# A two-layer attention and mixture-of-experts kernel: finer layernorm and exponential steps, routers called in fewer steps, and the first layer's tiles woven in from the third quarter

## The chip, the cores and the metric

The kernel runs on one core of one Trainium2 chip. The metric is the device time of one execution in microseconds (us). The kernel before took 978.13 us in the median of three runs (972.77 to 980.31).

## What is computed

All in float32. The input x has 16 x 256 tokens of 128 channels. Four residual steps follow one another, and each begins with a layernorm of x:

```python
x = x + attn_a(layernorm(x))   # 16 heads of 8, softmax inside blocks of 64 tokens
x = x + ffn(layernorm(x))      # router, top 2 of 8 experts, hidden 512, silu(g) * u
x = x + attn_b(layernorm(x))   # 16 heads over the 16 sequences of one position, plus a band bias
x = x + ffn(layernorm(x))      # the same experts again
```

The expert step needs, for each token, the two largest of eight router logits, a softmax over these two, and the two experts' outputs weighted by it.

## The kernel before, in words

**Tiling.** The 256 positions are cut in four quarters (q = 0 to 3). A quarter has 1024 tokens, which lie in SBUF as `xq[q]`, 8 groups of 128; a half is four groups. "Layer 0" is attn_a with its ffn, "layer 1" attn_b with its ffn. For each quarter a layer does its attention in two halves (`attention_a`, L397, or `attention_b`, L487), and after both halves a `router` (L585).

**Attention.** `prepare_a` and `prepare_b` make the layernorm, turn it on TensorE (PE), and make queries and keys. `attention_a` does for each group: values, then for two blocks scores on PE (L411), the row maximum (L419) and the subtraction (L420) on VectorE (DVE); then one exponential of both blocks on ScalarE (ACT, L425), transposes of the blocks (L430), their copies (L434), the product with the values (L441), the division, and an add into `xq` on GpSimd (POOL, L449). `attention_b` has the same order of work for a pair of groups, with one exponential at L535. `layernorm_t` (L266) is the layernorm of all: BN statistics of four groups, a power on POOL, the scaling of four groups, the transposes; it yields after each of these.

**Experts.** `router` makes logits, chooses two experts per token, counts, and gets each token's row in a table sorted by expert. It then scatters 16 x 128 rows to `sorted_in` in device memory by indirect DMAs of POOL (L694). `tile_tables` builds lists of tiles of 256 rows, each of one expert; it runs among the scatters. A list knows the rows of the first two quarters, the next one of the third, the last one of all. `experts` works through 39 tiles of a layer: fetch of rows (`xin`) and of three weight pieces (`w`) by SP two tiles ahead, transposes of the rows (`xt`, L889), the products g and u (L947), tanh (L952), two DVE operations (L953, L955), the product down (`acc`, L897), transposes and weighting, and a scatter to `results` (L920). Each tile is two units (`units`). `combine` reads `results` back and adds them to `xq`.

**Order of the work.** All these are Python generators. `weave(main, *sides)` steps through an attention half (24 steps in layer 0, 20 in layer 1) and calls the side generators in proportion: a side of `count` calls is spread over the first `n` steps. The sides are the router of the quarter before, the preparation of the next half, and units of experts. A scheduler below the kernel then settles each engine's final order from this program order and the dependencies. `behind_now` adds a dependency: a layernorm's or router's operation is put behind the last subtraction (`beat`) issued so far. In layer 0 units begin with quarter 3 (7 units by the end of its first half, 15 by the end of its second); the last router is run with a unit at every second call, and units then go on to number 52. In layer 1 units of layer 0 fill the first three quarters (`GOAL`), and layer 1's own begin behind quarter 2.

```python
CHOSEN = 10                       # the router's calls before its first scatter
ROUTER = CHOSEN + TOP * NG + 4    # 30 calls in all
sides = [(routing, ROUTER // 2 if half == 0 else ROUTER, n)]
```

Of the kernel before, what the change touches and what calls it, by code (L numbers as in the profile page):

```python
# [25 lines left out]
NQ = T // BS  # L26
# [4 lines left out]
TOP = 2  # L31
# [79 lines left out]
def hybrid_kernel(  # L111
# [154 lines left out]
    def layernorm_t(q, halves, name, put, keep=None, own=None):  # L266
        mv = p2.tile([P, NG, 2], F32, tag="mv", name=f"mv_{name}")
        rstd = p2.tile([P, NG], F32, tag="rstd", name=f"rs_{name}")
        ln = {}
        for half in halves:  # L270
            gs = range(4 * half, 4 * half + 4)
            stats = p2.tile([P, 4, 6], F32, tag="stats", name=f"st_{name}_{half}")
            for i, g in enumerate(gs):
                behind_now(nc.vector.bn_stats(out=stats[:, i, :], in_=xq[q][:, g, :]))
                nc.vector.bn_aggr(out=mv[:, g, :], in_=stats[:, i, :])
            some = slice(4 * half, 4 * half + 4)
            veps = p2.tile([P, 4], F32, tag="veps", name=f"ve_{name}_{half}")
            arrived[0] = nc.vector.tensor_scalar(veps, mv[:, some, 1], EPS, None, ALU.add).ins
            nc.gpsimd.tensor_tensor(rstd[:, some], veps, minus_half[:, some], ALU.pow)
            yield  # L280
        for half in halves:
            if keep is None:
                ln[half] = p2.tile([P, 4, C], F32, tag="ln", name=f"ln_{name}_{half}")
            for g in range(4 * half, 4 * half + 4):
                behind_now(
                    nc.vector.tensor_scalar(
                        ln[half][:, g % 4, :] if keep is None else keep(g),
                        xq[q][:, g, :], mv[:, g, 0:1], rstd[:, g : g + 1],
                        ALU.subtract, ALU.mult,
                    )  # L290
                )
            if own is not None:
                own(half)
            yield
        for half in halves:
            pt = psum(f"lnp_{name}_{half}")
            for i in range(4):
                g = 4 * half + i
                nc.tensor.transpose(
                    pt[:, i * P : (i + 1) * P],  # L300
                    ln[half][:, i, :] if keep is None else keep(g), ident,
                )
            put(half, pt)
            yield
# [92 lines left out]
    def attention_a(q, half):  # L397
        lnT, qT, kx = ready.pop((q, half))
        for g in range(4 * half, 4 * half + 4):
# [7 lines left out]
            for b in range(2):  # L407
                sc = ps_sc.tile([P, 512], F32, tag="sc", name=f"sc_{n}_{b}")
                blk = 2 * (g % 4) + b
                for v in range(2):  # L410
# [10 lines left out]
                    ex[:, b], sc3, mx[:, 0:8].unsqueeze(2).to_broadcast([P, 8, BS]),  # L421
                    ALU.subtract,
                ).ins
                yield
            nc.scalar.activation(ex, ex, AF.Exp)  # L425
            eT = p2.tile([P, 2, 4, P], F32, tag="eT", name=f"eT_{n}")
            for b in range(2):
                pt = psum(f"t_{n}_{b}")
# [58 lines left out]
    def attention_b(q, half):  # L487
# [15 lines left out]
        for dg in range(2 * half, 2 * half + 2):  # L503
# [7 lines left out]
            for gg in range(2):  # L511
# [3 lines left out]
                for j in range(4):  # L515
# [15 lines left out]
                beat[0] = nc.vector.tensor_tensor(  # L531
                    ex[:, gg], sb, mx.unsqueeze(2).to_broadcast([P, H, 32]), ALU.subtract
                ).ins
                yield
            nc.scalar.activation(ex, ex, AF.Exp)  # L535
            for gg in range(2):
                g = 2 * dg + gg
                n = f"B{q}_{g}"
# [313 lines left out]
    def experts(layer):  # L852
        def fetch(li, i):
# [9 lines left out]
                in_=sorted_in[layer][bass.ds(row, TT)].rearrange("(p b) r -> p (b r)", b=2),  # L863
            )
            known = [put for q in range(LISTED + li) for put in after[layer, q]]
            key = f"rows_{layer}"
            tc.declare_no_dep(
                got.ins, group=key, keep=known, reason="rows that the list did not know"
# [139 lines left out]
    def units(layer, upto):  # L1008
        while unit[layer] < upto:
            unit[layer] += 1  # L1010
            next(tiles[layer])
            yield

    def run(gen):
        for _ in gen:
            pass


    def weave(main, *sides):
        taken = [0] * len(sides)  # L1020
        for k, _ in enumerate(main):
            for i, (side, count, n) in enumerate(sides):
# [3 lines left out]
        for i, (side, count, n) in enumerate(sides):  # L1026
# [12 lines left out]
    FIRST = BEGIN[0] + BEGIN_B - 3  # L1039
    GOAL = [FIRST + (BEGIN[2] - FIRST) * (k + 1) // 3 for k in range(3)]  # L1040
    GOAL += [BEGIN[2] + (UNITS - BEGIN[2]) * (k + 1) // 3 for k in range(3)]

    for layer in range(2):
        tiles[layer], unit[layer] = experts(layer), 0
        if layer == 0:
            first = prepare_a(0, 0)
            next(first)
            for some in late:
                follow(some.ins, arrived)
            run(first)  # L1050
        else:
            weave(begin_b(0), (units(0, FIRST), FIRST - unit[0], BEGIN_B))
        routing = iter(())
        for q in range(NQ):
            for half in range(2):
                n = STEPS[layer]
                sides = [(routing, ROUTER // 2 if half == 0 else ROUTER, n)]
                last = (q, half) == (NQ - 1, 1)
                if layer == 0:
                    main = attention_a(q, half)  # L1060
                    if not last:
                        sides.append((prepare_a(q + half, 1 - half), 5, 2 * n // 3))
                else:
                    main = attention_b(q, half)
                    if half == 0:
                        sides.append((prepare_b(q, 1), 3, n // 2))
                    elif q < NQ - 2:
                        sides.append((begin_b(q + 1), BEGIN_B, 4 * n // 5))
                if q == NQ - 1:
                    goal = BESIDE * (1 + half) // 2  # L1070
                    goal = max(goal, unit[layer])
                    sides.append((units(layer, goal), goal - unit[layer], n))
                elif layer == 1:
                    goal = GOAL[2 * q + half]
                    sides.append((units(0, goal), goal - unit[0], n))
                weave(main, *sides)
                if layer == 1 and half == 1:
                    finish_b(q)
                    if q == NQ - 2:
                        n = BEGIN_B - 3  # L1080
                        run(routing)
                        weave(begin_b(q + 1), (units(1, n), n, BEGIN_B))
            run(routing)
            routing = router(layer, q)
# [49 lines left out]
```

## Time and profile before

| what | value |
|---|---|
| median of the runs, us | 978.13 (972.77 to 980.31, three runs) |
| the profiled execution's own time, us | 1056.63 |
| its span, us | 1054.9 |
| mean granted TensorE clock | 0.911 |
| PE busy | 901.1 us (85%) |
| DVE busy | 619.6 us (59%) |
| ACT busy | 397.6 us (38%) |
| POOL busy | 361.1 us (34%) |
| DMA moved | 107.69 MB, 102 GB/s in the mean |

The profile is of one execution. Busy time is the time in which an engine worked on an instruction. PE is TensorE's matmuls and PEld its weight loads, which overlap them; each float32 matmul is two records. PEclk is the share of full clock granted to TensorE. Idle time before an instruction is put down to what released it last. The first 330 us are layer 0's attention: quarters 1, 2 and 3 begin near 74, 156 and 235 us; the last router of layer 0 and its remaining tiles follow up to about 455 us. The adds into `xq` (L449) mark the ends of the groups.

### The profile page before, as it was taken

Reading aid. Unit: us, or ns where it says so; the run is one execution under the profiler, and the core shown is the slowest. Engines: PE = TensorE matmul, PEld = TensorE weight load, DVE = VectorE, ACT = ScalarE, POOL = GpSimd, SP = SyncE. Lnnn points to the kernel's source line nnn. Section 1 sums busy time; section 2 is a strip of 40 time slices with the busy share of each in tenths; the row PEclk is TensorE's granted clock in tenths of the full one; section 3 lists DMA queues with packets and bytes.
Section 4 is the critical chain, followed back from the end, with each engine's and each line's share of the span. In section 5 each row is a group of like instructions: output and inputs, shape, how many; then the busy total and the mean of one; then the engine's idle time right before and its main releaser. Section 6 shows DMA issues by size and latency. Waiting matters only on the chain.

```text
span 1054.9 us, 17640 instructions
## 1 busy us (share of the span) xinstructions
PE 901.1 (85%) x5992; PEld 733.6 (70%) x5992; DVE 619.6 (59%) x1749; ACT 397.6 (38%) x773; POOL 361.1 (34%) x404
## 2 busy tenths in 40 slices
PE   5987897989989979989887789588976997999993
PEld 3765666768778758877765667467765776887872
DVE  4676357557746745577766447546754674456452
ACT  2442243244434323436444254233622332443431
POOL 2121522442443463341112631442225345333322
PEclk9997787689989999999997889898978988999997
DMA  7000000041333545673121211133203444568772
GB/s 198 3 2 1 29 14 1 21 127 41 99 101 106 151 149 166 196 225 96 42 81 41 65 58 42 61 95 127 81 14 109 121 134 148 170 192 253 222 213 88
DMA packets 104922, 107.69 MB, mean 102 GB/s; under 512 B 10688, under 2 KB 80320, under 8 KB 104832
## 3 DMA queue, kind: packets, MB, share of 16 engines
q1 hardware_dynamic: 95024, 87.36, 27.8%
q0 software_dynamic: 9088, 18.89, 5.1%
q8 instruction: 48, 0.79, 0.3%
q10 hardware_dynamic: 720, 0.30, 0.1%
q14 instruction: 42, 0.34, 0.1%
HBM read 83.38 MB, written 23.13 MB: 101 GB/s over the span
## 4 chain that ended last, share of the span: by engine, by line
PE 66%; DVE 12%; DMA 6%; another core or an unknown queue 5%; ACT 5%; issue 4%; POOL 1%; SPq 1%; ACTq 0%; POOLq 0%; DVEq 0%
PE g L947 11%; PE acc L897 10%; PE u L947 10%; PE o_A L441 6%; PE sc_A L411 6%; PE t_A L430 3%; PE v_B L354 3%; PE o_B L554 2%; DMA back<-results 2%; PE sc_B L517 2%; DMA xin<-sorted_in 2%; DMA results<-yo,to 2%; PE v_A L354 2%; PE lg_F L599 1%
## 5 line engine op out<-in xcount | busy, mean ns | idle before, releaser
L920 POOL DMA_INDIRECT results<-yo,to x156 | 154.1, 988 | 299.7 <-ACT yo L913 269.3
L897 PE MATMUL acc<-h,w 128*128 128x256 f32 x624 | 174.3, 401 | 12.1 <-DVE h L955 9.1
L947 PE MATMUL g<-xT,w 128*128 128x256 f32 x624 | 171.5, 394 | 4.4 <-issue 2.7
L947 PE MATMUL u<-xT,w 128*128 128x256 f32 x624 | 169.8, 393 | 3.8 <-DVE th L953 2.0
L952 ACT ACTIVATE th<-g 128x512 f32<-128x512 f32 x156 | 93.6, 600 | 203.8 <-PE g L947 132.1
L953 DVE SCALAR_TENSOR_TENSOR th<-th,g 128x512 f32<-128x512 f32 x156 | 106.4, 683 | 105.6 <-ACT th L952 84.0
L694 POOL DMA_INDIRECT sorted_in<-rows,pos_i_F x128 | 125.0, 977 | 124.7 <-issue 38.4
L897 PEld LDWEIGHTS acc<-h,w 128*128 128x128 f32 x624 | 121.6, 200 | 36.4 <-DVE h L955 14.8
L947 PEld LDWEIGHTS g<-xT,w 128*128 128x128 f32 x624 | 119.0, 198 | 23.0 <-issue 4.9
L947 PEld LDWEIGHTS u<-xT,w 128*128 128x128 f32 x624 | 115.7, 196 | 20.4 <-issue 3.4
L955 DVE TENSOR_TENSOR h<-th,u 128x512 f32<-128x512 f32 x156 | 106.6, 684 | 21.6 <-remote 5.6
L411 PE MATMUL sc_A<-k_A,q_A 128*128 128x256 f32 x256 | 86.4, 456 | 19.0 <-DVE ex_A L420 14.1
L441 PEld LDWEIGHTS o_A<-va,eT_A 128*64 128x64 f32 x1024 | 63.6, 147 | 20.4 <-issue 8.4
L411 PEld LDWEIGHTS sc_A<-k_A,q_A 128*128 128x128 f32 x256 | 50.8, 225 | 33.2 <-DVE ex_A L420 16.3
L441 PE MATMUL o_A<-va,eT_A 128*64 128x18 f32 x1024 | 67.7, 219 | 5.6 <-issue 3.1
L905 ACT COPY yT<-acc 128x256 f32<-128x256 f32 x78 | 29.0, 372 | 100.6 <-PE acc L897 89.2
L419 DVE TENSOR_REDUCE mx_A<-sc_A 128x8 f32<-128x512 f32 x64 | 43.1, 681 | 35.5 <-PE sc_A L411 34.8
L434 ACT COPY eT_A<-t_A 128x512 f32<-128x512 f32 x64 | 36.6, 589 | 67.9 <-PE t_A L430 61.8
L449 POOL TENSOR_TENSOR xq<-xq,att_A 128x128 f32<-128x128 f32 x32 | 14.6, 456 | 130.5 <-DVE att_A L373 120.1
L913 ACT ACTIVATE yo<-y,xin 128x128 f32<-128x128 f32 x156 | 48.6, 366 | 20.4 <-PE y L908 10.6
L425 ACT ACTIVATE ex_A<-ex_A 128x1024 f32<-128x1024 f32 x32 | 34.0, 1064 | 42.5 <-DVE ex_A L420 31.0
L430 PEld LDWEIGHTS t_A<-k_sb,ex_A 128*128 128x128 f32 x256 | 34.0, 159 | 20.7 <-issue 10.4
(173 smaller groups left out, 1318.0 us busy)
## 6 DMA issues: line engine op xcount, KB each, us to landing
w<-in_wg SPq DMA_DIRECT2D x78, 256.0 KB
w<-in_wu SPq DMA_DIRECT2D x78, 256.0 KB
w<-in_wd SPq DMA_DIRECT2D x78, 256.0 KB
xin<-sorted_in SPq DMA_DIRECT2D x78, 132.0 KB
back<-results SPq DMA_DIRECT2D x16, 512.0 KB
results<-yo,to POOLq DMA_INDIRECT x156
sorted_in<-zero SPq DMA_DIRECT2D x2, 1056.0 KB
sorted_in<-rows,pos_i_F POOLq DMA_INDIRECT x128
```

Of the source, the lines that this page charges most:

```text
L354: nc.tensor.matmul(pv[:, a * P : (a + 1) * P], lhsT=src[:, g * n + a].rearrange("p r k -> p (r k)"), rhs=w, start=True, stop=True,)
L411: nc.tensor.matmul(sc[:, v * 4 * BS : (v + 1) * 4 * BS], lhsT=qT[:, blk, 2 * v : 2 * v + 2, :].rearrange("p r k -> p (r k)"), rhs=kx[:, :, ...
L430: nc.tensor.transpose(pt[:, i * P : (i + 1) * P], ex[:, b, 2 * i : 2 * i + 2, :].rearrange("p h k -> p (h k)"), ident,)
L441: nc.tensor.matmul(po[b * BS : (b + 1) * BS, i * 18 : (i + 1) * 18], lhsT=eT[:, b, 2 * v + i % 2, u * BS : (u + 1) * BS], rhs=vt[:, b, 2 * ...
L694: put_row = nc.gpsimd.indirect_dma_start(out=sorted_in[layer], out_offset=bass.IndirectOffsetOnAxis(ap=pos_i[:, k, g : g + 1], axis=0), in ...
L897: nc.tensor.matmul(acc[:, 0:TT], lhsT=w[:, 2, hc * P : (hc + 1) * P], rhs=h[:, j * TT : (j + 1) * TT], start=(hc == 0), stop=(hc == NHC - 1),)
L913: nc.scalar.activation(y[:, b, :], py[:, b * P : (b + 1) * P], AF.Identity, scale=t[:, b, C : C + 1],)
L920: put_row = nc.gpsimd.indirect_dma_start(out=results[layer], out_offset=bass.IndirectOffsetOnAxis(ap=to[:, b : b + 1], axis=0), in_=y[:, b ...
L947: nc.tensor.matmul(p[:, j * TT : (j + 1) * TT], lhsT=w[:, k, hs], rhs=xT, start=True, stop=True,)
L952: nc.scalar.activation(th, pg, AF.Tanh, scale=0.5)
L953: nc.vector.scalar_tensor_tensor(th, th, 1.0, pg, ALU.add, ALU.mult)
L955: beat[0] = nc.vector.tensor_tensor(h, th, pu, ALU.mult).ins
```

## The change

`layernorm_t` yields after two groups of statistics and after two groups of scaling, where it yielded after four. The exponentials of `attention_a` and `attention_b` are made for each block right after its subtraction, where one instruction covered two blocks. `weave` takes a first and a last step for each side. The router has 34 calls in place of 30 (the layernorm has four more); 25 are made beside the first half (15 before) and 9 in the first third of the second half. The preparation of a half of layer 0 has 7 calls for 5, `begin_b` 15 for 11. Units of layer 0 begin in the second half of quarter 2, from its 12th step on: 3 by its end, 8 and 13 by the ends of quarter 3's halves (before: 0, 7 and 15). In layer 1 the two halves of quarter 3 have the goals 8 and 13 (before 8 and 15).

```diff
@@ layernorm_t
-            for i, g in enumerate(gs):
+            for i in range(4):
+                g = 4 * half + i
                 behind_now(nc.vector.bn_stats(out=stats[:, i, :], in_=xq[q][:, g, :]))
                 nc.vector.bn_aggr(out=mv[:, g, :], in_=stats[:, i, :])
+                if i == 1:
+                    yield
...
-            for g in range(4 * half, 4 * half + 4):
+            for i in range(4):
+                g = 4 * half + i
                 behind_now(
                     nc.vector.tensor_scalar(
...
                 )
+                if i == 1:
+                    yield
@@ attention_a
                     ALU.subtract,
                 ).ins
+                nc.scalar.activation(ex[:, b], ex[:, b], AF.Exp)
                 yield
-            nc.scalar.activation(ex, ex, AF.Exp)
@@ attention_b
+                nc.scalar.activation(ex[:, gg], ex[:, gg], AF.Exp)
                 yield
-            nc.scalar.activation(ex, ex, AF.Exp)
@@ the plan
-    CHOSEN = 10
+    CHOSEN = 14
...
-                while taken[i] < min(count * (k + 1) // n, count):
+                while taken[i] < min(count * max(k + 1 - first, 0) // (last - first), count):
...
-    BEGIN_B = 2 + 6 + 3
-    FIRST = BEGIN[0] + BEGIN_B - 3
+    BEGIN_A, BEGIN_B = 5 + 2, 2 + 10 + 3
+    AHEAD = 8
+    FAST = ROUTER * 3 // 4
+    FIRST = BEGIN[0] + AHEAD
...
+    OWN = {5: BESIDE // 4, 6: BESIDE * 5 // 8, 7: BESIDE}
...
-                sides = [(routing, ROUTER // 2 if half == 0 else ROUTER, n)]
...
-                if q == NQ - 1:
-                    goal = BESIDE * (1 + half) // 2
+            if half == 0:
+                sides = [(routing, FAST, 0, n)]
+            else:
+                sides = [(routing, ROUTER - FAST, 0, n // 3)]
+            if layer == 0:
+                main = attention_a(q, half)
+                if hq + 1 < 2 * NQ:
+                    sides.append((prepare_a((hq + 1) // 2, 1 - half), BEGIN_A, 0, 2 * n // 3))
+                wanted, goal = 0, OWN.get(hq, 0)
...
+                wanted, goal = (0, GOAL[hq]) if q < NQ - 1 else (1, OWN[hq])
+            goal = max(goal, unit[wanted])
+            first = n // 2 if layer == 0 and hq == 5 else 0
+            sides.append((units(wanted, goal), goal - unit[wanted], first, n))
+            weave(main, *sides)
```

More of the change, by code (lines that the diff above doesn't have):

```diff
@@ L270, in layernorm_t @@
         for half in halves:
-            gs = range(4 * half, 4 * half + 4)
             stats = p2.tile([P, 4, 6], F32, tag="stats", name=f"st_{name}_{half}")
-            for i, g in enumerate(gs):
+            some = slice(4 * half, 4 * half + 4)
+            for i in range(4):
+                g = 4 * half + i
                 behind_now(nc.vector.bn_stats(out=stats[:, i, :], in_=xq[q][:, g, :]))
                 nc.vector.bn_aggr(out=mv[:, g, :], in_=stats[:, i, :])
-            some = slice(4 * half, 4 * half + 4)
+                if i == 1:
+                    yield
             veps = p2.tile([P, 4], F32, tag="veps", name=f"ve_{name}_{half}")
@@ L283, in layernorm_t @@
                 ln[half] = p2.tile([P, 4, C], F32, tag="ln", name=f"ln_{name}_{half}")
-            for g in range(4 * half, 4 * half + 4):
+            for i in range(4):
+                g = 4 * half + i
                 behind_now(
                     nc.vector.tensor_scalar(
-                        ln[half][:, g % 4, :] if keep is None else keep(g),
+                        ln[half][:, i, :] if keep is None else keep(g),
                         xq[q][:, g, :], mv[:, g, 0:1], rstd[:, g : g + 1],
@@ L865, in fetch @@
             known = [put for q in range(LISTED + li) for put in after[layer, q]]
+            assert len(known) == (LISTED + li) * TOP * NG
             key = f"rows_{layer}"
@@ L1021, in weave @@
         for k, _ in enumerate(main):
-            for i, (side, count, n) in enumerate(sides):
-                while taken[i] < min(count * (k + 1) // n, count):
+            for i, (side, count, first, last) in enumerate(sides):
+                while taken[i] < min(count * max(k + 1 - first, 0) // (last - first), count):
                     taken[i] += 1
                     next(side, None)
-        for i, (side, count, n) in enumerate(sides):
+        for i, (side, count, _, _) in enumerate(sides):
             for _ in range(count - taken[i]):
@@ L1047, in hybrid_kernel @@
             next(first)
+            next(first)
             for some in late:
@@ L1051, in hybrid_kernel @@
         else:
-            weave(begin_b(0), (units(0, FIRST), FIRST - unit[0], BEGIN_B))
+            weave(begin_b(0), (units(0, FIRST), FIRST - unit[0], 0, BEGIN_B))
         routing = iter(())
-        for q in range(NQ):
-            for half in range(2):
-                n = STEPS[layer]
-                sides = [(routing, ROUTER // 2 if half == 0 else ROUTER, n)]
[L1058 to L1068, printed above, removed]
-                if q == NQ - 1:
-                    goal = BESIDE * (1 + half) // 2
[L1071 to L1082, printed above, removed]
@@ new lines, in hybrid_kernel @@
+        n = STEPS[layer]
+        for hq in range(2 * NQ):
+            q, half = hq // 2, hq % 2
+            if half == 0:
[7 more added lines that the diff above has]
+                wanted, goal = 0, OWN.get(hq, 0)
+            else:
+                main = attention_b(q, half)
+                if half == 0:
+                    sides.append((prepare_b(q, 1), 3, 0, n // 2))
+                elif q < NQ - 2:
+                    sides.append((begin_b(q + 1), BEGIN_B, 0, 4 * n // 5))
+                wanted, goal = (0, GOAL[hq]) if q < NQ - 1 else (1, OWN[hq])
[3 more added lines that the diff above has]
+            weave(main, *sides)
+            if half == 0:
+                continue
@@ L1083, in hybrid_kernel @@
             run(routing)
+            if layer == 1:
+                finish_b(q)
+                if q == NQ - 2:
+                    weave(begin_b(q + 1), (units(1, AHEAD), AHEAD, 0, BEGIN_B))
             routing = router(layer, q)
```

## The prediction, made before the changed kernel was run

> **What bounds the kernel now.** I read the page's first two parts, then the table by stretches, the groups, PE's own waits and the timeline. The page says which engine fills the span and what it was granted:
>
> ```profile
> PE 901.1 (85%) x5992; PEld 733.6 (70%) x5992; DVE 619.6 (59%) x1749; ACT 397.6 (38%) x773; POOL 361.1 (34%) x404
> PEclk9997787689989999999997889898978988999997
> ```
>
> TensorE (PE) is the bound, but its clock falls below full in slices 4 to 8. The profiled execution took 1056.63 us (span 1054.9), 78.5 us over the median of 978.13. In its chain of waits 4.9%, some 52 us, is put on "another core or an unknown queue"; one core runs, so I take this and the cold clock after it for the profile's own cost. The first such piece starts at 126.5 us; what lies before it should be in the timed runs too. The table by stretches (length; busy PE, PEld, DVE, ACT, POOL; clock; DMA) gives attention halves of layer 0:
>
> ```profile
> 48.50:74.30 25.80, 23.67 (x215) 18.08 (x213) 17.22 (x50) 11.54 (x17) 4.08 (x6) 1.00 0.00 1
> 74.30:123.70 49.40, 40.46 (x254) 30.93 (x253) 27.26 (x95) 15.12 (x22) 14.31 (x17) 0.72 0.03 11
> 155.80:205.30 49.50, 40.48 (x253) 31.21 (x252) 31.32 (x123) 15.14 (x22) 13.24 (x15) 0.72 0.03 9
> 205.30:234.50 29.20, 26.41 (x212) 20.19 (x211) 17.17 (x51) 11.64 (x17) 14.43 (x17) 0.88 0.38 119
> 234.50:282.40 47.90, 46.48 (x337) 38.42 (x336) 35.92 (x121) 21.61 (x39) 15.15 (x18) 1.00 0.16 51
> 403.00:458.00 55.00, 55.00 (x273) 48.24 (x272) 27.54 (x47) 22.58 (x59) 18.99 (x20) 1.00 0.61 187
> ```
>
> A half alone takes 25.8 us. A half beside a router (rows two and three) has 39 more matmul records and takes 23.6 us more. At clock 0.72, 28% of the time is missing: 0.28 x 49.4 = 13.8 us. Idle grows from 2.1 to 8.9 us; the rest, 3.0 us, is the router's own matmuls. With expert tiles beside it (row five) the same work runs at clock 1.00. PE's waits name the idle:
>
> ```profile
> PE sc_A L411 <- DVE ex_A L420: 14.1, 13, 3.2
> PE t_B L541 <- ACT ex_B L535: 4.7, 2, 4.5
> PE rank_F L662 <- DVE runs L649: 3.4, 1, 3.4
> PE rank_F L662 <- issue: 3.3, 1, 3.3
> ```
>
> and the timeline shows two such holes, the scores held by VectorE (DVE) and the ranks held by the router's chain:
>
> ```profile
> 86.40 2.93 PE L411 MATMUL sc_A<-k_A,q_A 128*128 128x256 f32 x6 [2.49 <-DVE ex_A L420]
> 102.50 0.66 PE L662 MATMUL rank_F<-taken_F,k_late 128*128 128x64 f32 x2 [3.34 <-issue]
> ```
>
> [...] after the 3.34 us hole at 99.2 the same 4 transposes take 1.06 us at 106.0, against 0.60 at 98.6. [...]
>
> **A: exponentials block by block.** Removed: 32 ACTIVATEs of 1064 ns (L425) and 16 of 1059 (L535). Added: 96 of half the size. The tanh of 128x512 (L952) takes 600 ns, so a pair costs 1200: (1200 - 1062) x 48 = 6.6 us more on ACT, hidden since ACT is busy 38%. Without that cover it would be 6.6 us of the end at most. Gain: the first block's transposes no longer wait for the second subtract (684 ns) and half the exponential (464 ns), so start 1.15 us earlier. That matters only where PE is waiting: in the order in which the built programs' instructions stand, t_A_1_0 now stands before the last matmul of sc_A_2_0, in the 2.49 us hole, and there are two such holes. Some 1 us each, and 1 us of the 4.5 us wait of t_B: -3 us. Bounds: 0, and -14 (the waits for ex_A and ex_B, 18.8 us, three quarters gone).
>
> **B: layernorms by two groups.** No instruction is added; four groups' BN statistics are 4 x (272 + 165) ns = 1.7 us, now in runs of 0.9. In the built order the first router has 26 instructions between mx_A_1_0 and the subtract that follows it before, 28 after: that burst (76.0 to 81.1 us) isn't shortened. But the subtract of the second block of group 0 now stands ahead of two groups' statistics, and two ln rows move behind two subtracts. I take 0.4 us in each of 8 routers: -3 us; bounds 0 and -8. That finer steps do no more is what I read from the order.
>
> **C: routers in fewer groups.** CHOSEN 10 to 14 is the same work in more calls, so ROUTER is 34 for 30. The first half makes 25 calls in place of 15, so 11 scatters in place of 5, at 962 ns and 0.30 us between: 6 x 1.26 = 7.6 us of POOL move forward. Behind them on POOL stand the adds of att into xq (455 ns), which nothing needs before the next router. DVE's choice takes 14/25 x 24 = 13.4 steps of attention in place of 10/15 x 24 = 16. The rank hole: in the new order no PE work stands between v_A_2 and rank, while before k_A_1 and t_A_2_0 (1.06 + 0.60 us) did. DVE's va, 0.42 us, then about 16 links of the chain follow v_A_2; 17 links with four k_A and a va took 5.1 us at 97.3 (3.05 without those), so 0.18 each and 2.9 us. With 0.38 us from v to va the hole is about 3.7 us against 3.34. The four k_A (0.42 us each in sequence) now stand behind the router's positions, covered by q_A's scaling on ACT (2.79 us); uncovered, 1.7 us. Sum: +1 us over the routers of quarters 0 and 1; bounds -4 and +10.
>
> **D: tiles beside the third quarter.** Pair-steps (units) of layer 0 go from 0, 7, 8, 15 (last half of quarter 2, two halves of quarter 3, last router) to 3, 5, 5, 17. A tile takes 5.07 us in the dense stretch (ten from 402.8 to 453.5), so a unit 2.54. PE's work is the same; the gain is what falls into idle time. Quarter 2's last half has 2.8 us idle and 0.12 x 29.2 = 3.5 us lost to clock: I take 3. Two more units beside the last router fall into its 10.0 us idle (330 to 403): 3. The new risk: xt of tile 0 now stands near t_A_6. Its rows need all 32 scatters. Four of these stand after the add of group 4, which was at 211.8 us: 5.1 us, 2.5 to land (220.4 to 223.0 before), one xin fetch 2.1 (issued 223.1, used 225.3): 221.5, against about 222 for t_A_6. No slack, so +1 for a stall. SP's later fetches (two tiles ahead) and weights come sooner by as much; only tile loads are queued there. Sum -5; bounds -12 and +8.
>
> **E: cold clock.** From 14 to 330 us the missing clock is 0.28 x 49.4 + 0.16 x 32.1 + 0.28 x 49.5 + 0.12 x 29.2 + 0.07 x 47.7 = 40 us. The rank holes stay, so the cold stretch behind each stays. I take a fifth of the rest, 36 us, for A and B together beyond the 3.5 in D: -7. Bounds: +6 and -30.
>
> **F: layer 1.** begin_b has 15 steps for 11, the units beside it are the same 8; the order hardly changes: -1; bounds -10 and +10.
>
> Sum: -3 -3 +1 -5 -7 -1 = -18 us. In the profiled execution's time 1056.6 - 18 = 1039; against the median 978.1 - 18 = 960 us.
>
> **The rivals.** (1) The cold stretches of the two router quarters go altogether: for this speaks row five, clock 1.00 with the same router; against it the rank hole. Another 20 us of E: 940. (2) The holes only move: the burst of 26 to 28 instructions stays, dense stretches stay at 55.00 of 55.00; it does not do what it says, and A and D alone leave 975. (3) Slower: the compressed routers. If DVE's denser choice lengthens the hole per router by the uncovered k_A, 1.7 us, and draws one more 6.8 us cold stretch (3.4 lost) in the six routers that run beside attention: 6 x 5.1 = +31, against -18 gives +13: 991. It decides from 3 us per router. Against it: DVE is busy 27.3 of 49.4 us there.
>
> **How the numbers follow.** My forecast has 0.45, its own range 948 to 970; rival 1 0.22, rival 2 0.20, rival 3 0.13. The 8-in-10 range reaches from 936 (rival 1, with A at its far bound) to 989. A measurement can tell about 1%, 968.3 to 987.9. Faster: 0.43 + 0.22 + 0.02 = 0.67. Same: 0.02 + 0.17 + 0.03 = 0.22. Slower: 0.01 + 0.10 = 0.11.
>
> **What would show it.** A: twice the exponentials, near 600 ns, and t_A or t_B less often behind ACT. B: waits of sc_A for ex_A below 14.1 us. C: rank_F still waiting over 3 us in quarters 1 and 2. D: g of tile 0 before the last half of quarter 2 ends, xt's wait for xin there under 3 us, clock there 1.00. E: mean clock above 0.911, router halves under 47 us. Wrong: a stall at the first xt over 5 us, router halves longer than 49.5 us, or rank holes gone.

## The result

| what | before | after |
|---|---|---|
| median, us (20 runs each, same series) | 981.26 (972.77 to 988.16) | 974.12 (970.42 to 978.74) |
| ratio | | 0.9925 [0.9905, 0.9945] |
| profiled execution, us | 982.37 | 974.5 |
| its span, us | 980.6 | 972.7 |
| mean granted TensorE clock | 0.942 | 0.949 |

The change makes the kernel 0.75% faster, some 7 us. The forecast was 18 us. Ratios in this document leave out executions more than 1.5% above the fastest of the same kernel, so a ratio can differ from that of the two medians. The profile that the forecast was read from was of an execution 78 us longer than the timed runs; the kernel was profiled again (run before_again), and that execution of 982.37 us is the "before" of this section and the next.

### The profile page after: what moved, and what is told of

It reads as the page before. It is cut to its first block, busy times and chain, and to the rows that moved or that the text cites. A ratio compares the mean times of both kernels' runs of the same rounds, so it can differ in the third digit from the quotient of the medians.

```text
span 972.7 us, 17640 instructions
## 1 busy us (share of the span) xinstructions
PE 856.2 (88%) x5992; PEld 706.9 (73%) x5992; DVE 619.7 (64%) x1749; ACT 402.2 (41%) x821; POOL 358.6 (37%) x404
## 4 chain that ended last, share of the span: by engine, by line
PE 68%; DVE 11%; DMA 8%; ACT 5%; POOL 3%; issue 3%; SPq 0%; ACTq 0%; POOLq 0%; DVEq 0%
PE g L953 12%; PE u L953 11%; PE acc L903 11%; PE o_A L446 6%; PE sc_A L416 5%; DMA back<-results 3%; PE t_A L435 3%; PE v_B L359 2%; PE o_B L559 2%; PE sc_B L522 2%; DMA results<-yo,to 2%; POOL sorted_in L699 2%; PE v_A L359 2%; DMA sorted_in<-rows,pos_i_F 2%; ACT q_A L333 2%
## 5 line engine op out<-in xcount | busy, mean ns | idle before, releaser
L903 PE MATMUL acc<-h,w 128*128 128x256 f32 x624 | 166.2, 385 | 6.4 <-DVE h L961 6.2
L953 PE MATMUL u<-xT,w 128*128 128x256 f32 x624 | 165.3, 384 | 3.8 <-DVE th L959 3.8
L953 PE MATMUL g<-xT,w 128*128 128x256 f32 x624 | 166.3, 386 | 0.9 <-ACT xT L897 0.5
L903 PEld LDWEIGHTS acc<-h,w 128*128 128x128 f32 x624 | 116.7, 192 | 26.3 <-DVE h L961 10.4
L953 PEld LDWEIGHTS g<-xT,w 128*128 128x128 f32 x624 | 117.0, 193 | 17.3 <-issue 1.6
L953 PEld LDWEIGHTS u<-xT,w 128*128 128x128 f32 x624 | 112.3, 192 | 18.9 <-DVE th L959 6.0
L416 PE MATMUL sc_A<-k_A,q_A 128*128 128x256 f32 x256 | 80.1, 423 | 20.4 <-DVE ex_A L425 13.1
L416 PEld LDWEIGHTS sc_A<-k_A,q_A 128*128 128x128 f32 x256 | 45.8, 206 | 30.4 <-DVE ex_A L425 12.4
L429 ACT ACTIVATE ex_A<-ex_A 128x512 f32<-128x512 f32 x64 | 40.1, 634 | 47.0 <-DVE ex_A L425 46.7
L359 PE MATMUL v_B<-wi_sb,xt_B 128*128 128x128 f32 x256 | 37.0, 298 | 24.0 <-DVE att_B L378 23.1
```

The costliest lines, as they stand in the source:

```text
L359: nc.tensor.matmul(pv[:, a * P : (a + 1) * P], lhsT=src[:, g * n + a].rearrange("p r k -> p (r k)"), rhs=w, start=True, stop=True,)
L416: nc.tensor.matmul(sc[:, v * 4 * BS : (v + 1) * 4 * BS], lhsT=qT[:, blk, 2 * v : 2 * v + 2, :].rearrange("p r k -> p (r k)"), rhs=kx[:, :, ...
L903: nc.tensor.matmul(acc[:, 0:TT], lhsT=w[:, 2, hc * P : (hc + 1) * P], rhs=h[:, j * TT : (j + 1) * TT], start=(hc == 0), stop=(hc == NHC - 1),)
L953: nc.tensor.matmul(p[:, j * TT : (j + 1) * TT], lhsT=w[:, k, hs], rhs=xT, start=True, stop=True,)
```

## The profile after

First the busy shares and the granted clock in 40 slices, from the page of the kernel before, profiled again:

```profile
PE 861.1 (88%) x5992; PEld 708.5 (72%) x5992; DVE 620.2 (63%) x1749; ACT 397.3 (41%) x773; POOL 360.1 (37%) x404
PEclk9998998699999999999998879997999999999997
```

and from the page of the changed kernel:

```profile
PE 856.2 (88%) x5992; PEld 706.9 (73%) x5992; DVE 619.7 (64%) x1749; ACT 402.2 (41%) x821; POOL 358.6 (37%) x404
PEclk9999879789999999999999879989999999999997
```

The work is the same: 5992 matmul records, 48 more ACTIVATEs and 4.9 us more of them on ACT. Both pages have their weak places where layer 0 runs beside its routers (slices 4 to 9) and where layer 1 does so (slices 22 to 24). The table by stretches (length; busy PE, PEld, DVE, ACT, POOL; clock; DMA share; GB/s) gives for the kernel before the four halves of quarters 1 and 2 of layer 0, and then the second quarter of layer 1:

```profile
73.50:118.00 44.50, 34.88 (x258) 26.75 (x258) 28.41 (x102) 15.61 (x23) 14.31 (x16) 0.88 0.03 11
118.00:146.50 28.50, 24.82 (x204) 18.16 (x204) 16.48 (x45) 11.45 (x17) 13.09 (x16) 0.94 0.07 24
146.50:194.90 48.40, 39.28 (x252) 31.05 (x253) 31.44 (x126) 15.22 (x22) 13.23 (x15) 0.75 0.03 9
194.90:220.80 25.90, 23.59 (x213) 17.72 (x211) 17.53 (x50) 11.53 (x17) 14.40 (x17) 1.00 0.33 108
...
517.70:600.40 82.70, 63.27 (x571) 52.19 (x570) 51.25 (x153) 32.72 (x54) 30.56 (x30) 0.86 0.16 52
```

and for the changed kernel the same stretches:

```profile
77.60:119.20 41.60, 33.72 (x281) 26.05 (x279) 28.00 (x105) 15.92 (x27) 19.11 (x22) 0.92 0.06 19
119.20:150.60 31.40, 27.07 (x187) 20.51 (x186) 16.13 (x39) 12.09 (x20) 8.18 (x12) 0.84 0.03 11
150.60:195.20 44.60, 37.65 (x261) 29.20 (x259) 31.29 (x132) 16.08 (x27) 16.11 (x18) 0.81 0.04 13
195.20:228.90 33.70, 30.38 (x224) 23.98 (x223) 17.82 (x44) 14.02 (x25) 11.17 (x14) 0.90 0.32 99
...
516.50:596.20 79.70, 60.07 (x558) 49.78 (x557) 49.13 (x151) 33.09 (x59) 29.50 (x30) 0.85 0.18 54
```

In quarters 1 and 2 the first halves became 3 to 4 us shorter and the second halves 3 to 8 us longer; the sum of the four is 147.3 us before and 151.3 after. Quarter 3, which has ten units of tiles beside it for fifteen, went from 90.1 to 81.9 us. Layer 0 as a whole, to the first read of its results, took 419.7 us and takes 421.9. Layer 1's attention went from 348.5 to 336.7 us, and its second quarter is still a stretch with a clock of 0.85 and 19.6 us without matmul. TensorE's own waits in the changed kernel (total, times, longest, us) say what stands there:

```profile
PE v_B L359 <- DVE att_B L378: 23.1, 2, 12.6
...
PE rank_F L667 <- DVE runs L654: 3.5, 1, 3.5
PE rank_F L667 <- issue: 3.5, 1, 3.5
```

against these in the kernel before:

```profile
PE lnp_B L299 <- DVE vb L360: 10.5, 1, 10.5
...
PE ot_B L495 <- DVE att_B L373: 8.2, 2, 6.2
...
PE t_B L541 <- ACT ex_B L535: 4.6, 2, 4.5
...
PE rank_F L662 <- DVE runs L649: 3.4, 1, 3.4
PE rank_F L662 <- issue: 2.9, 1, 2.9
```

The two rank holes of layer 0 (TensorE's waits for what the ranks are counted from) stayed: 2.9 and 3.4 us before, 3.5 us each after. The wait for the exponential of two blocks (t_B, 4.5 us) is gone. And two waits in layer 1, of 10.5 and 6.2 us, became two of 12.6 and 10.5. These last two are named v_B <- att_B, but att_B is short work (0.29 us): what was late is seen one engine further, in the timeline. Lines of it for the changed kernel around both waits, engine by engine:

```profile
545.09 0.96 POOL L699 DMA_INDIRECT sorted_in<-rows,pos_i_F  x1 [5.90 <-DVE pos_i_F L692]
...
564.02 0.96 POOL L699 DMA_INDIRECT sorted_in<-rows,pos_i_F  x1 [0.30 <-DMA sorted_in<-rows,pos_i_F]
565.00 1.05 POOL L281 TENSOR_TENSOR rs_B<-ve_B,minus_half 128x4 f32<-128x4 f32 x1
...
548.27 0.27 DVE L280 TENSOR_SCALAR ve_B<-mv_B 128x4 f32<-128x4 f32 x1
...
566.09 1.28 DVE L289 TENSOR_SCALAR ln_B<-xq,mv_B,rs_B 128x128 f32<-128x128 f32 x4 [10.07 <-POOL rs_B L281]
...
571.50 2.05 PE L359 MATMUL v_B<-wi_sb,xt_B 128*128 128x128 f32 x8 [12.63 <-DVE att_B L378]
...
651.21 0.16 DVE L924 TENSOR_TENSOR to<-xin,no_pads 128x2 int32<-128x2 f32 x1 [11.60 <-DMA xin<-sorted_in]
...
652.64 2.05 PE L359 MATMUL v_B<-wi_sb,xt_B 128*128 128x128 f32 x8 [10.49 <-DVE att_B L378]
```

The variance of the next quarter's layernorm (ve_B) is ready at 548.5 us. Its power (rs_B) starts on POOL at 565.0, because 16 scatters of the router stand before it, 0.96 us each and 0.30 between, some 20 us from 545.1. VectorE's scaling waits 10.07 us for the power and then 2.34 us for that of the second half, the attention's att_B stands behind both in VectorE's order, and TensorE waits 12.63 us for att_B. The second wait has another head: `to`, which a tile makes from its fetched rows, stands early in VectorE's order and waits 11.60 us for a fetch of layer 1's first tile. That fetch needs the last scatter of the next router, which starts on POOL at 646.58 us; SP issues the fetch at 649.05.

The kernel before has the same first wait under another name (lnp_B <- vb). There 12 of the 16 scatters stand before the first power; the second one, for which VectorE waits 6.14 us more, starts at 572.29 behind three others and two scatters of a tile. Lines of its timeline:

```profile
563.88 0.96 POOL L694 DMA_INDIRECT sorted_in<-rows,pos_i_F  x1 [0.31 <-issue]
564.86 1.05 POOL L279 TENSOR_TENSOR rs_B<-ve_B,minus_half 128x4 f32<-128x4 f32 x1
...
573.37 2.94 DVE L286 TENSOR_SCALAR ln_B<-xq,mv_B,rs_B 128x128 f32<-128x128 f32 x4 [6.14 <-POOL rs_B L279]
```

## The experiments

In the expectations, "GpSimd queue" (theory 1 in the first eight) is the theory that bunched scatters hold what stands behind them on GpSimd, and that the routers' fast pace so gives the gain of the other parts back. "Holes only move" (theory 2) is its rival: the waits belong to VectorE's own chains and go elsewhere when one is removed. Ratios are against the kernel before on the same chip, with 95% intervals.

| run | median, us | ratio |
|---|---|---|
| exp_alone | 976.74 | 0.9934 [0.9911, 0.9957] |
| layernorm_alone | 965.54 | 0.9818 [0.9769, 0.9867] |
| pace_alone | 998.39 | 1.0162 [1.0107, 1.0217] |
| tiles_alone | 991.56 | 1.0089 [1.0059, 1.0120] |
| exp_and_layernorm | 954.69 | 0.9709 [0.9658, 0.9760] |
| fast_pace_without_tiles | 977.72 | 0.9946 [0.9924, 0.9969] |
| after_old_pace | 954.24 | 0.9750 [0.9691, 0.9809] |
| after_old_pace_layer1 | 963.62 | 0.9833 [0.9782, 0.9885] |
| after_to_behind | 965.92 | 0.9859 [0.9807, 0.9912] |
| fast_pace_power_on_vector | 969.30 | 0.9763 [0.9693, 0.9833] |
| slow_choice_fast_scatters | 978.27 | 0.9980 [0.9959, 1.0001] |
| old_choice_fast_scatters | 1035.52 | 0.9901 [0.9867, 0.9936] |
| old_choice_fast_scatters_2 | 972.04 | 0.9893 [0.9859, 0.9927] |
| old_pace_to_behind | 955.47 | 0.9701 [0.9653, 0.9749] |
| exp_layernorm_to_behind | 953.83 | 0.9684 [0.9636, 0.9731] |
| exp_layernorm_to_behind_power | 948.92 | 0.9661 [0.9621, 0.9701] |
| exp_layernorm_to_behind_power_all | 949.54 | 0.9679 [0.9641, 0.9718] |

**before_again** is the kernel before, with a new profile.

> The kernel before, profiled once more, since its first profile was 78 us longer than its runs. Theory 1 (the queue of GpSimd: the changed routers bunch 16 scatters, DVE then waits for a power or for a tile's rows behind them, 23 us of PE idle time in two places) expects a span near 980 us without a PE wait over 6 us in layer 1. Theory 2 (holes only move: the kernel before has waits of the same kind and sum) expects 15 us or more of PE waits behind scatters in layer 1 here too. Both expect the two rank holes of 3.4 us near 99 and 181 us.

982.37 us. The 10.5 us wait is there, so "no wait over 6 us in before" of the GpSimd-queue view was a miss: the wait isn't new with the change, it became 2 us longer.

**The old pace**, everywhere or in layer 1 alone:

```diff
-            if half == 0:
-                sides = [(routing, FAST, 0, n)]
-            else:
-                sides = [(routing, ROUTER - FAST, 0, n // 3)]
+            sides = [(routing, ROUTER // 2 if half == 0 else ROUTER, 0, n)]
```

> The changed kernel with the routers at their old pace (half of the calls beside the first half, the rest over the first half of the second). Theory 1 expects 945 to 962 us, ratio 0.965 to 0.98 to before: the 12.6 and 10.5 us waits of v_B shrink by more than half. Theory 2 expects the time of the changed kernel within 0.5%, 969 to 979 us.

> The changed kernel with the old pace in layer 1 alone. Theory 1, both waits lie in layer 1: 945 to 962 us, within 0.4% of the run with the old pace everywhere. If the fast pace costs or gains in layer 0, the two runs differ by more. Theory 2: 969 to 979 us.

954.24 and 963.62 us. The fast pace costs the changed kernel some 17 us (0.9925 to 0.975), about 9 of them in layer 1. The intervals of the two old-pace runs overlap, so layer 0's share of some 8 us is less sure; the GpSimd-queue view had expected 0.4% between the two at most, a miss. In the trace of the first both rank holes of layer 0 and the 12.6 us wait are gone. The second wait, which that view expected to shrink by more than half, stayed at 9.5 us.

**The tile's places behind.** The changed kernel, with `to` tied to the last subtraction issued (the expectation calls it the product h):

```diff
-                nc.vector.tensor_tensor(to, t[:, :, C + 1], elsewhere, ALU.max)
+                behind_now(nc.vector.tensor_tensor(to, t[:, :, C + 1], elsewhere, ALU.max))
```

> The changed kernel with one dependency more: DVE's operation that reads a tile's row numbers (to, from xin) is put behind the last product h, so it can't stand early in DVE's queue and hold it until xin lands. Theory 1 expects the 10.5 us wait at 642 us to go and 6 to 16 us to be won: 958 to 968 us. Theory 2 expects another wait in its place and no gain: 970 to 979 us.

965.92 us. The 10.5 us wait at 642 us is gone and that quarter of layer 1 takes 57.9 us for 70.7; a new wait of 6.5 us (u for th) comes at 667 us. So `to` was the head of the second wait, and more than half of it moved on.

**One part alone**, on the kernel before: the exponentials, the layernorms (with CHOSEN 14), the fast pace (22 of 30 calls in the first half, 8 in the first third of the second), the early tiles (goals 3, 9 and 15, since a shorter router leaves 15 where the change has 3, 8 and 13).

> The kernel before with the exponentials made block by block, and nothing else. The prediction had -3 us for this (bounds 0 and -14). Theory 1 expects 0.990 to 1.000 of before. Theory 2 (holes move) expects 0.997 to 1.003.

> The kernel before with layernorms in steps of two groups (and the call counts that go with it), nothing else. The prediction had -3 us (bounds 0 and -8), and -7 us of clock with the exponentials. Theory 1 expects 0.990 to 1.000, theory 2 0.997 to 1.003.

> The kernel before with the routers' calls bunched: 22 of 30 beside the first half, 8 in the first third of the second. Theory 1 (bunched scatters make DVE wait in layer 1) expects a loss of 8 to 30 us, ratio 1.008 to 1.03. The prediction had +1 us, 1.001 (bounds -4 and +10). Theory 2 expects 0.995 to 1.005.

> The kernel before with units of layer 0 from the second half of quarter 2 on (3, 9 and 15 by the ends of the halves), the routers at their old pace, layernorms and exponentials as before. The prediction had -5 us (bounds -12 and +8): 0.988 to 1.000. Theory 2 expects 0.995 to 1.003. If the first tile's rows hold PE, its wait at the first xt is over 3 us.

-6.5, -18, +16 and +9 us. The layernorms alone are the largest gain, and not where they were thought to be: layer 0 takes 420.3 us for 419.7, while layer 1's second quarter takes 69.9 for 82.7. Layer 0's two rank holes are gone too, and TensorE is without matmul there for 39.2 us in place of 43.9; but in this execution it was at half clock for 68 us in place of 44. The row of layer 1's second quarter in the table by stretches has clock 0.98 for 0.86:

```profile
516.50:586.40 69.90, 58.55 (x570) 48.37 (x570) 50.08 (x152) 32.65 (x54) 29.81 (x30) 0.98 0.21 62
```

and its timeline of POOL says why:

```profile
543.70 1.05 POOL L281 TENSOR_TENSOR rs_B<-ve_B,minus_half 128x4 f32<-128x4 f32 x1 [8.84 <-DVE ve_B L280]
549.18 1.01 POOL L281 TENSOR_TENSOR rs_B<-ve_B,minus_half 128x4 f32<-128x4 f32 x1 [4.44 <-DVE ve_B L280]
551.12 1.04 POOL L698 DMA_INDIRECT sorted_in<-rows,pos_i_F  x1 [0.94 <-DVE pos_i_F L691]
```

With smaller steps both powers stand before the first scatter. The 10.5 us wait is gone.

The fast pace alone loses in another way than it does on top of the other parts. In its trace TensorE is without matmul for 116.6 us, against 119.5 in the kernel before, and the two waits of layer 1 are shorter, 5.0 and 5.5 us. What grew is the time lost to the clock, 0.068 x 991.4 = 67 us against 0.058 x 980.6 = 57; and ranks wait 2.3 to 3.2 us in five quarters, where they waited so in two. So the +16 us is not shown to come from GpSimd's queue.

**The fast pace with the power elsewhere.** The changed kernel; the power of layer 1's attention layernorms is made by VectorE. The scatters stay where they are.

```diff
-            nc.gpsimd.tensor_tensor(rstd[:, some], veps, minus_half[:, some], ALU.pow)
+            if name[0] == "B":
+                nc.vector.tensor_scalar(guess, veps, -0.47, 1.51, ALU.mult, ALU.add)
+                for step in range(2):
+                    nc.vector.scalar_tensor_tensor(part, guess, -0.5, guess, ALU.mult, ALU.mult)
+                    nc.vector.tensor_tensor(part, part, veps, ALU.mult)
+                    nc.vector.scalar_tensor_tensor(better, part, 1.5, guess, ALU.add, ALU.mult)
...
+            else:
+                nc.gpsimd.tensor_tensor(rstd[:, some], veps, minus_half[:, some], ALU.pow)
```

> The whole change, but the power of the layernorms of layer 1's attention (two per quarter) is made by VectorE in seven small operations (a linear start and two Newton steps, exact to 2e-5 on these variances) in place of one on GpSimd. The routers keep the fast pace, and all 16 scatters of the first router of layer 1 still stand together in GpSimd's queue; only what stood behind them and what VectorE waited for is gone. GpSimd queue: the 12.6 us wait of TensorE near 559 us goes with the half-clock stretch behind it, the second quarter of layer 1's attention takes some 70 us for 79.7, and the time is 962 to 966 us (ratio 0.981 to 0.985). Holes only move (the fast pace hurts through VectorE's own chain): the wait comes back elsewhere in that quarter, and the time stays at 971 to 979 us. The rank holes of 3.5 us in layer 0 stay under both.

0.9763 [0.9693, 0.9833], below the whole change's interval. But three of its six executions, 973.66 to 975.54 us, are not in this ratio, and the median of all six is 969.30 us: the forecast of 962 to 966 lies between, and the size of the gain is uncertain. The stage itself is clearer. Its second quarter of layer 1:

```profile
517.60:585.10 67.50, 59.87 (x571) 49.12 (x570) 49.73 (x166) 32.20 (x58) 28.21 (x28) 0.92 0.22 64
```

67.5 us for 79.7, and no wait there over 2.8 us, with all 16 scatters together on POOL as before. This shows it for this quarter: the scatters hurt there through the power queued behind them. The second wait, headed by `to`, stayed (10.6 us). The rank holes of layer 0 (3.5 and 3.54 us) stayed, as expected.

**With and without tiles.** exp_and_layernorm is both singles on the kernel before; fast_pace_without_tiles adds the pace to that.

> The kernel before with the exponentials by block and the layernorms by two groups; routers at the old pace, tiles as before. It is the kernel of the old-pace run without the early tiles. GpSimd queue: the early tiles cost 9 us alone only because they fell on a layer 0 with cold stretches and rank holes; where these are gone they cost nothing, so this kernel is at 0.975, 955 to 959 us. The other view, that the early tiles cost their 9 us in any company: ratio 0.963 to 0.968, 945 to 950 us.

> The whole change without its early tiles: exponentials by block, layernorms by two groups, routers at the fast pace, the first tiles with quarter 3 as before. If the early tiles cost nothing in the change's company: within 3 us of the changed kernel, ratio 0.989 to 0.996. If they cost their 9 us there too: 0.980 to 0.986. If they gain there (they fill halves that the fast routers have left): 0.997 to 1.004.

954.69 and 977.72 us. So the change adds up in this order: layernorms and exponentials together -28 us (0.9709 of 982.88), the pace +23 (0.9709 to 0.9946, of 982.9), the tiles -2 (0.9946 to 0.9925, intervals overlapping), sum -7. Between the profiled executions of exp_and_layernorm and fast_pace_without_tiles the pace's cost lies in layer 1's second quarter (68.4 to 79.3 us) and in layer 0 (409.9 to 425.9 us), there with no more time without matmul (43.0 and 41.4 us) but 58 us at half clock for 34. The early tiles, with goals a little higher, cost 9 us on the kernel before and nothing that can be measured within the change. At the old pace (0.9709 without them, 0.975 with) the intervals overlap too.

**What opens the rank holes of layer 0.** In slow_choice_fast_scatters the choice (14 calls) takes 20 steps of the first half, nearly the old pace, and the rest comes in the first third of the second half.

```diff
+            if layer == 0 and half == 0:
+                sides = [(routing, CHOSEN, 0, 5 * n // 6)]
+            elif layer == 0:
+                sides = [(routing, ROUTER - CHOSEN, 0, n // 3)]
-            if half == 0:
+            elif half == 0:
```

> The whole change, but in layer 0 the 14 calls of a router before its first scatter are spread over the first 20 steps of the half beside it, as at the old pace, and the 20 calls with the scatters all come in the first third of the next half. Layer 1 keeps the fast pace. Two reasons for the 3.5 us rank holes of layer 0 stand against each other. Pace of the choice (the ranks' matmuls come up in TensorE's order right behind v_A_2, while VectorE has 17 links still to make): the rank holes go, and the time falls by what the old pace is worth in layer 0, 9 to 10 us, to 962 to 967 us (ratio 0.981 to 0.986). Bunched scatters (GpSimd is what holds layer 0 too): the time stays at 972 to 978 us, with waits of VectorE for GpSimd in the second halves.

978.27 us, 0.998: neither reason. The holes are still there, 3.3 and 3.4 us, 13 to 15 us later. Its timeline has the copy of the logits and the rank at

```profile
106.96 0.21 DVE L616 COPY lgs_F<-lg_F 128x64 f32<-128x64 f32 x1
...
113.71 0.69 PE L667 MATMUL rank_F<-taken_F,k_late 128*128 128x64 f32 x2 [3.27 <-DVE taken_F L651]
```

and the timeline of after_old_pace, where the two programs' earlier work runs within 0.1 us of each other, at

```profile
97.30 0.23 DVE L616 COPY lgs_F<-lg_F 128x64 f32<-128x64 f32 x1 [0.85 <-PE lg_F L604]
...
105.97 0.43 PE L667 MATMUL rank_F<-taken_F,k_late 128*128 128x64 f32 x2
```

The router's logits are ready at 97.3 us in both. At the old pace the copy and the choice behind it fill the time in which VectorE would wait for the next scores, and the rank is ready long before TensorE comes to it. In the other kernel the copy was issued one step later, so `behind_now` tied it to a later subtraction, 10 us on, and VectorE was idle for 6.3 us in between. Up to the 20th step the calls differ by one, at the 17th. old_choice_fast_scatters takes that call back and keeps the scatters bunched:

```diff
-                sides = [(routing, CHOSEN, 0, 5 * n // 6)]
+                sides = [(routing, ROUTER // 2, 0, n)]
             elif layer == 0:
-                sides = [(routing, ROUTER - CHOSEN, 0, n // 3)]
+                sides = [(routing, ROUTER - ROUTER // 2, 0, n // 3)]
```

> As the slow-choice run, but in the first half layer 0's routers take exactly the old pace's calls (17 over 24 steps), and the other 17 calls with their scatters all come in the first third of the next half. Against the slow-choice run this moves one call of the choice one step, from the 18th to the 17th; the copy of the logits then stands behind the subtraction before TensorE's wait for the queries, and not behind the one after it. Layer 1 keeps the fast pace. If the place of the choice in VectorE's order makes the rank holes: both holes go (no wait of rank over 1 us in layer 0), and the time is 963 to 968 us (ratio 0.982 to 0.987). If the bunched scatters cost in layer 0: no rank holes, but 972 to 979 us all the same.

> The same kernel as in the run before it, whose measurement fell into an hour in which the kernel before took 1046 us. Its trace had no rank hole in layer 0. If the place of the choice in VectorE's order is what costs: 963 to 968 us against a kernel before near 982 (ratio 0.982 to 0.987). If the bunched scatters cost in layer 0: 972 to 979 us.

The first of the two had 1035.52 us against 1046.28 of the kernel before in that series, all of it longer than in every other series; the second had 972.04, 0.9893. In both traces no rank waits as long as 0.5 us in layer 0, so the tie of that one call made the holes of the slow-choice run. But the time is what the bunched-scatters reason expected. TensorE's waits between 74 and 320 us in the second run say where it went:

```profile
PE sc_A L416 <- DVE ex_A L425: 21.0, 7, 8.6
PE lnp_A L304 <- DVE ln_A L289: 6.0, 1, 6.0
```

Behind both stand powers of the preparations (rs_A), for which VectorE waits 14.3 us in all, against 8.0 in after_old_pace and 5.0 in the changed kernel. So the fast pace in layer 0 was seen to wait in either of two ways: for a choice tied too late, or for powers behind the scatters. What each costs was not separated. Layer 1's waits of 12.6 and 10.6 us stand in this run as in the changed kernel.

**Better versions.** The two waits of layer 1 taken away at the old pace, with and without early tiles; then the power of layer 1, and of both layers' attention, on VectorE.

> The old-pace kernel with one more edit: the operation that makes a tile's places from its fetched rows stands in VectorE's queue behind the subtractions issued so far. GpSimd queue: the 9.5 us wait of TensorE near 628 us goes, as the same edit took a 10.5 us wait and 8 us of time from the whole change, and the time is 944 to 949 us (ratio 0.962 to 0.967). Holes only move: the wait is replaced by others of the same sum, 952 to 957 us (0.972 to 0.977).

> Exponentials by block and layernorms by two groups on the kernel before, with the tile's places behind the subtractions; no early tiles, routers at the old pace. GpSimd queue: within 3 us of the old-pace kernel with the same edit, 944 to 950 us. If early tiles cost their 9 us in any company: 935 to 941 us.

> Exponentials by block and layernorms by two groups at the old pace and without early tiles, the tile's places behind the subtractions, and the power of layer 1's layernorms on VectorE. GpSimd queue: at the old pace the powers stand ahead of the scatters already, so the last edit saves only what is left of the 12.9 us of TensorE's idle in the second and third quarter of layer 1: 0 to 4 us, 948 to 954 us (ratio 0.964 to 0.969). Holes only move: seven small operations more per half on VectorE cost 2 to 5 us, 0.970 to 0.975.

> Exponentials by block and layernorms by two groups at the old pace, no early tiles, the tile's places behind the subtractions, and the power of the layernorms of both layers' attention on VectorE (the routers' own layernorms keep theirs on GpSimd). It tests GpSimd's queue as the reason in layer 0 too: there the power of a preparation waits behind scatters (VectorE waits 10.2 us in all for it in the kernel with the power of layer 1 alone moved), and TensorE's waits of 3.5 us near 122 and 6.1 us near 185 follow. GpSimd queue: both waits go, and the time falls by 5 to 9 us, to 939 to 945 us (ratio 0.956 to 0.962). Holes only move: other waits take their place, 947 to 952 us (0.964 to 0.969).

955.47, 953.83, 948.92 and 949.54 us. The best measured, 0.9661 [0.9621, 0.9701], is half of the change plus two edits; it beats both kernels by 2.6% or more, but its interval overlaps with exp_and_layernorm's. `to` behind brings 6 to 7 us on the whole change (0.9925 to 0.9859, intervals that just touch) and nothing that can be measured at the old pace. From exp_and_layernorm to exp_layernorm_to_behind TensorE's idle in the third quarter of layer 1 falls from 13.3 to 3.8 us, and the fourth quarter grows from 96.6 to 104.5, so there the rival was right. In the last run layer 0's waits of 3.5 and 6.1 us went as expected, the idle of layer 0 fell from 41.8 to 31.8 us, and the time did not move: a miss. Quarter 2's first half in the run with layer 1's power alone,

```profile
146.80:184.00 37.20, 31.25 (x276) 25.38 (x275) 28.50 (x117) 15.51 (x27) 11.08 (x13) 0.95 0.02 7
```

and in the run with both:

```profile
138.60:182.20 43.60, 39.18 (x244) 31.07 (x243) 26.37 (x103) 14.55 (x25) 10.12 (x12) 0.69 0.02 7
```

The idle went from 6.0 to 4.4 us, and the clock from 0.95 to 0.69. The gain was eaten by the clock, and not in this one execution alone: the six executions of the last run have mean clocks of 0.935 to 0.950, median 0.9445, those of the run before it 0.949 to 0.959, median 0.9545. One hundredth of 948 us is 9.5 us, about as much as the idle removed. The two runs were on different chips, but the kernel before had a median clock of 0.937 on both.

## Why the prediction was right or wrong

The direction was right, the size was not: -18 us forecast, -7 measured, nearest to rival 2's -3 (975 from 978). That the sum came so near is luck. A, B and the clock that E gave them were forecast at -13 and measured -28 together; C was forecast at +1 and measured +23 on top of them; the two errors went opposite ways.

**A, exponentials: right in mechanism, half in size.** -3 forecast within 0 to -14, -6.5 measured alone. The exponentials take 634 and 631 ns, for 600 taken from the tanh row. The wait of t_B for ex_B, of which 1 us was to go, went whole (4.6 us to none), and no wait of sc_A for ex_A is over 1.6 us, where two were 3.4; the two rank holes grew to 4.1 and 4.2 us, which the sum did not have.

**B, layernorms: the gain that was sized too small.** -3 forecast, bounds 0 and -8; -18 measured alone. The failing step is the sentence "That finer steps do no more is what I read from the order". It looked at VectorE's burst in layer 0. Some 13 of the 18 us are in layer 1's second quarter, and come from another engine: the finer steps let two powers pass ahead of 16 scatters. That they also take away the rank holes of layer 0 was not foreseen; why they do was not tested apart from the calls that change with them.

**C, routers: the step that failed.** Forecast +1, bounds -4 and +10; measured +16 alone and some +23 on top of A and B. On top of them some 11 of it are layer 1's second quarter, where the scatters again stand before the powers. The sum counted 7.6 us of scatters moved forward and said that behind them stand adds "which nothing needs before the next router". That is so for the adds, and the powers that stand in the same queue were put at nothing. The rank hole was well worked out (3.7 us forecast, 3.5 measured), but set against the hole of before and not against the kernel with A and B alone, where the holes are gone: the pace brings them back. That two such holes cost layer 0 much was not shown. A step must be costed on top of the other steps.

**D, tiles: right in company, wrong alone.** -5 forecast within -12 and +8; -2 within the change, not resolved, and +9 alone, with slightly higher goals. No wait of the first xt for its rows of 2 us or more stands in the changed kernel; in tiles_alone the first one is 2.5 us, the stall that D gave +1 for. The clock of 1.00 that D named as its sign for quarter 2's last half did not come: 0.90 there.

**E, cold clock: the sum right, the place wrong.** -7 forecast for layer 0. Lost clock over the span is 0.058 x 980.6 = 56.9 us before and 0.051 x 972.7 = 49.6 after: -7. But in these two executions layer 0 spends 44 us at half clock in both, and the gain is in layer 1.

**F, layer 1: "the order hardly changes" failed.** -1 forecast, bounds -10 and +10. Layer 1's attention became 11.8 us shorter in the profiled executions, while its two long waits grew.

**The reading of the profile.** The 52 us on "another core or an unknown queue" were taken for the profile's own cost. In the second profile of the same kernel the chain could be followed back only to 655 us, in the changed kernel's it is whole, and neither names such a part; so the excess was no part of the timed runs, as taken; nor is it the cost of every profile, since the second has none of it. But that profile hid the wait that decided. VectorE waits in it for a power of layer 1's attention (rs_B) for 0.6 us in all, in the second profile for 10.4. The order in POOL's queue was the same in both, 12 scatters before the power; in the first, VectorE stood for 8.36 and 5.52 us just before, on waits that the timeline puts on "remote", so that almost nothing was left to wait for the power. So a list of waits could not have led to it, and a list of what stands in the queue could.

**The rivals.** Rival 1 fails with the holes. Rival 2 has the time and for the rank holes the mechanism (they stayed); its reason, that B does not do what it says, was wrong by 15 us, and C hid it. Rival 3 had C's direction and, in the whole change, not its way: the holes grew by 0.6 and 0.1 us and not by 1.7. In the pace alone it was nearer: ranks waited in five quarters, and 10 us more were lost to the clock.

**Open.** How layer 0's share of the pace's cost, some 8 of 17 us, splits between the late choice, the powers and the clock; and what decides the clock of a half with little idle.

## What to carry to other kernels

Before moving a run of instructions on an engine, list everything that stands behind them in its queue and who waits for it: here 1.05 us of power behind 20 us of scatters cost its quarter of layer 1 12 us (79.7 against 67.5). Cost each part of a change on top of the other parts, for a part can create the gain that the next one takes away; and when a change of several parts moves little, measure the parts alone. Where a dependency is tied to "the last one issued", a call one step later is another dependency.

## What the runs showed of the hardware

The half-clock stretches in the traces of layer 0 have lengths of 3.4, 6.8, 10.2, 13.7, 17.1, 20.5 and 23.9 us, each within 0.1 us of a multiple of the shortest, 3.41. Their sum varies between executions of kernels that differ in layer 0 by the place of `to` at most: 34.1 us (exp_and_layernorm), 37.5 (exp_layernorm_to_behind_power) and 58.0 (exp_layernorm_to_behind), with TensorE's idle at 43.0, 41.8 and 41.8 us, and the layer took 409.9, 412.1 and 419.1 us. What sets the lengths, and why the sums differ at nearly the same idle, was not shown. An idle microsecond removed was here worth anything from nothing (exp_layernorm_to_behind_power_all: 10.0 us less idle in layer 0, 949.54 us for 948.92) to more than itself (after_old_pace: 9.7 us less idle in layer 1's second quarter, 11.2 us less time).

Half clock also came without a long idle stretch before it. In exp_layernorm_to_behind_power_all no wait of TensorE between 74 and 320 us is over 2.5 us, and it is at half clock there for 54.6 us; the longest stretch, 23.9 us from 162.0 on, follows 6.8 us with 0.4 us of idle, by the matmul ends that the profile models. In the profile that the prediction was read from, the two rank holes, 3.34 and 3.39 us up to 102.5 and 184.2 us, each have half clock beside them, 17.1 us from 101.9 and from 183.8 on. That such a hole is the cause was the author's estimate and was not shown.
